# A sandwich layer (attention, then a ternary feed-forward) on one core: the feed-forward's splits turned by VectorE and HBM, two V units and one product moved, identity transposes at the start

## The chip, the cores and the metric

The kernel runs on one core of a Trainium2 chip. The metric is device time in microseconds (us) of one execution. Before the change it is 1528.37 us, the median of 3 runs (1528.33 to 1528.66).

## What is computed

The input x has two batches of 1024 rows of 512. W_Q, W_K and W_V have 16 heads of 128 x 512, W_O 16 of 512 x 128; w1 and w3 are 1365 x 512, w2 is 512 x 1365. All are fp32.

```python
def ternary_quant(w):
    s = mean(abs(w))
    return clip(round(w / s), -1, 1) * s          # as far as the value goes

def attn(x):                                      # causal, 16 heads of 128
    q, k, v = (einsum('bsd,hed->bhse', x, W) for W in (W_Q, W_K, W_V))
    s = einsum('bhse,bhme->bhsm', q, k) / sqrt(128), masked above the diagonal
    return einsum('bhse,hde->bsd', softmax(s) @ v, W_O)

def ffn(x):
    return (silu(x @ w1q.T) * (x @ w3q.T)) @ w2q.T   # w1q = ternary_quant(w1), ...

x = x + layernorm(attn(layernorm(x)))
out = x + layernorm(ffn(layernorm(x)))
```

## The kernel before, in words

**Numbers.** TensorE multiplies in a fast fp32 form of reduced precision, so most operands are split into a leading and a low part (and in attention a third, their difference form), and a product is the sum of two or three matmuls. Such parts are called forms here: `xb` are those of x, `qa`, `ql`, `qd` (also k, v, o) those of the weights, `za`, `zl`, `zd` those of the heads' outputs, `gh`, `gl` those of the hidden values. Scores (L555) and products with V (L649) run in plain fp32, which is two instructions for each.

**Start (L674 to L712).** The loads of x and of the first weights go out. VectorE and ScalarE normalise the rows of batch 0, tile by tile of 128 rows. `block_unit` (L392) turns a tile: four TensorE transposes against the identity (L402) into PSUM, then ScalarE (L406), VectorE (L407) and VectorE or POOL (L408) make its three forms. The first four tiles go through, then the query and key units of head 0 (L461), then V units.

**Attention.** There are N = 32 heads (16 in each batch), two to a pair g, with 8 steps i each, one for each tile of 128 query rows. The order is written out by hand in the loop at L796. Step i issues the scores of three steps ahead (`look`, L771: L555, causal mask L560, row maximum L564, exp L571, scaling L577), fill work for the next head (query and key units L470 and L477, V units L498, output units L518), and a product with V. A V unit (`value_unit`, L487) does two of the eight tiles of a pair in 24 matmuls of 256 columns; there are four for a pair. For a product, P must be transposed: VectorE turns blocks of 32 x 32 (L603), the blocks go to HBM (`hop<-blocks`, L614) and come back at their places in four reads (`pt<-hop`, L630). Two steps are turned together: product (n, m) covers steps 2m and 2m+1 of head n, and `product` (L767) says at which step it is issued: two steps after the second of them, three where that is step 7. In the last head the steps run in the order 4, 5, 6, 7, 0, 1, 2, 3, and the first three hidden units of the feed-forward are put in at steps 2, 4 and 6 (`early_hidden`, L777).

Raw weights come by `load_raw` (L414). The raw tile of V has the buffer of the difference form `vd` (tag "vd"), and those of Q and K the buffers of `qd` and `kd`. All DMAs are issued by SyncE in one queue, in order (SPq in the profile): a DMA that waits holds up those behind it. L835 loads the raw V of the next pair at step 1, L438 and L439 make its forms at steps 3 and 4, L445 at steps 5 and 6.

**Feed-forward.** There are four blocks (b, tb) of 512 rows, each with NF = 11 steps f over the hidden size. In step f the loop at L991 issues the hidden unit of two steps ahead (`hidden`, L309: 16 matmuls L317, Silu L325, VectorE L328, gh by ScalarE L333, gl by VectorE L334), then the down product of step f (L915: 8 matmuls into four PSUM accumulators), and three pieces of `middle`, the closing of batch 1's attention (in block 1 only). The block's input must be split ahead of its first hidden unit, which is issued at step 9 of the block before. `split_unit` does that for one tile of 128 rows at steps 4, 6, 7 and 8: load of the row tile (batch 0, L237), normalisation by VectorE (L123), four TensorE transposes into PSUM (L255), leading part by ScalarE (L257), low part by VectorE (L258). Block 1's splits were done in head N-2 in the same way. PSUM tiles named `mm` (tag "mm", four buffers) are shared by hidden units, splits, products and V units. After step 10, `finish` normalises the four sums, adds the residual (POOL, L939; for batch 0 from `res` loads) and stores out.

`tc.issue_after(i)` and `past(i)` put what follows behind instruction i in the order in which the program issues.

Of the kernel before, what the change touches and what calls it, by code (L numbers as in the profile page):

```python
# [9 lines left out]
FP = mybir.dt.float32  # L10
# [25 lines left out]
def sandwich_kernel(  # L36
# [85 lines left out]
    def normalise(dst, src, mv, r, t):  # L122
        return nc.vector.tensor_scalar(  # L123
            dst, src, mv[:, t, 0:1], r[:, t : t + 1], ALU.subtract, ALU.mult
        )
# [103 lines left out]
    def split_units(b, tb, t, stage):  # L229

        tt = tb * QT + t
        held = {}

        def load():
            held["x"] = xt = stage.tile([P, D], FP, name="xt")
            if b == 0:
                nc.sync.dma_start(xt, mid0[ts(tt, P), :])  # L237

        def normal():
            src = held["x"] if b == 0 else acc[:, tt, :]  # L240
            normalise(held["x"], src, mv_mid[b], r_mid[b], tt)

        return load, normal, lambda: split_turn(b, tb, t, held["x"])

# [92 lines left out]
    with ExitStack() as att:  # L337
# [91 lines left out]
        def lead_and_low(kind, n, part, first=False):  # L429

            if (kind, n) not in weights:
                weights[kind, n] = [form(kind, "a"), form(kind, "l")]
            lead, low = (w[:, part] for w in weights[kind, n][:2])
            raw = wraw[kind, n][:, part]
            if first:
                nc.vector.tensor_scalar(lead, raw, LEAD, None, ALU.mult)
            else:
                nc.scalar.mul(lead, raw, LEAD)  # L438
            nc.gpsimd.tensor_tensor(low, raw, lead, ALU.subtract)  # L439

        def difference_form(kind, n, part):
            if len(weights[kind, n]) == 2:
                weights[kind, n].append(form(kind, "d"))
            lead, low, diff = (w[:, part] for w in weights[kind, n])
            nc.vector.scalar_tensor_tensor(diff, low, -T12, lead, ALU.mult, ALU.add)  # L445
# [235 lines left out]
        @contextmanager  # L681
        def past(*instructions):
            with ExitStack() as order:
                for i in instructions:
                    order.enter_context(tc.issue_after(i.ins))
                yield

        def normal_pair(t):
            for k in (t, t + 1):
                row_stats(mv_in[0][:, k, :], acc[:, k, :])  # L690
            std_unit(0, t, 2)
            return [normal_unit(0, k) for k in (t, t + 1)]

        with past(*normal_pair(0)):
            done = normal_pair(2)
        with past(*done):
            for kind in range(2):
                lead_and_low(kind, 0, EVERY, first=True)
            blocks = [block_unit(0, t) for t in range(QT)]
        lead, low, diff = blocks[-1]  # L700
        with past(diff):
            for kind in range(2):
# [64 lines left out]
        product = {}  # L767
        for at, (n, i) in enumerate(order):
            if i % 2 == 1:
                product[at + (3 if i == NT - 1 else 2)] = n, i // 2  # L770
        def look(idx):  # L771
            if idx < len(order):
                live[order[idx]] = scores(*order[idx])
# [22 lines left out]
        for n in range(N):  # L796
            g, j = divmod(n, 2)
            b, pr = divmod(g, NP)

            fill = [[] for _ in range(NT)]  # L800

            def put(steps, units):
                for i, u in zip(steps, units):
                    fill[i].append(u)

            if n + 1 < N:
                units = [
                    lambda k=k, kind=kind: query_key_unit(n + 1, kind, k)()
                    for k in range(2)
                    for kind in range(2)  # L810
                ]
                late = {2 * NP - 1: (6, 7), N - 2: (5, 5)}.get(n, (5, 6))
                put((3, 4) + late, units)
            if j == 1 and g + 1 < G:
                units = [lambda u=u: value_unit(g + 1, u) for u in range(QT)]
                put((0, 1, 6, 7) if n != 2 * NP - 1 else (0, 1, 5, 6), units)
            if n == 0:
                put((1, 7), [lambda u=u: value_unit(0, u) for u in (2, 3)])
            if j == 0 and g > 0:
                outs = output_units(g - 1)  # L820
                put((0, 0, 0, 1, 4, 5, 6, 7), outs)
            for t in range(NT):
                if divmod(block_at + t, NT)[0] == n:
                    put([(block_at + t) % NT], [lambda t=t: block_unit(1, t)])
            for t in range(QT):
                if divmod(split_at + t, NT)[0] == n:
                    put([(split_at + t) % NT], splits[t][2:])
            if n == N - 1:
                put((2, 4, 6), [lambda f=f: early_hidden(f) for f in range(EARLY)])
            for i in range(NT):  # L830
                idx = n * NT + i
                with behind("turn", of=idx + 1):
                    if n + 2 < N and i > 5:
                        load_raw(i - 6, n + 2)
                    if j == 0 and g + 1 < G and i == 1:  # L835
                        load_raw(2, g + 1)
                    if j == 1 and i == 1:
                        load_raw(3, g)
                    if n == N - 2 and i >= NT - EARLY:
                        f = i - NT + EARLY  # L840
                        load_t13(f, wpool.tile([P, 2, D], FR, name=("va", "vd", "vl")[f]))
                todo = fill[i]
                for u in todo[:2]:
                    with past(newest[0]):
                        u()
                rest = None
                if idx in product:
                    with past(newest[0]):
                        rest = values(*product.pop(idx))
                for u in todo[2:]:  # L850
                    with past(newest[0]):
                        u()

                with behind("max", "half", "exp", of=idx + 1):
                    if n + 1 < N and i in (2, 3):
                        difference_form(i - 2, n + 1, EVERY)
                    if n + 1 < N and i in (1, 2):
                        lead_and_low(i - 1, n + 1, EVERY)
                    at = g + 1 - j
                    if at < G and i in (3, 4):  # L860
                        lead_and_low(2 + j, at, (FRONT, BACK)[i - 3])
                    if at < G and i in (5, 6):
                        difference_form(2 + j, at, (FRONT, BACK)[i - 5])
                with past(newest[0]):
                    look(idx + AHEAD)
                if rest:
                    with behind("max"):
                        rest()
                if idx + 2 < len(order):
                    with behind("max"):  # L870
                        turn(*order[idx + 2])
                        if idx + 3 == len(order):
                            bring(*next(iter(blocks_of)))
                with behind("max", "half", "turn"):
                    for u in side[idx]:
                        u()
# [8 lines left out]
    with ExitStack() as ffn:  # L885
# [56 lines left out]
        def finish_last(b, tb, t):  # L942
# [18 lines left out]
            for u in (t, t - 1) if t == QT - 1 else (t - 1, t):  # L961
# [7 lines left out]
                eng.tensor_tensor(y, y, acc[:, tt, :], ALU.add)  # L969
                nc.sync.dma_start(out[b, ts(tt, P), :], y)  # L970

        last = {}
        square = small.tile([P, 1], FP, name="square", bufs=1)
        nc.vector.tensor_tensor(square, scales[2][:, 2:3], scales[2][:, 2:3], ALU.mult)
# [15 lines left out]
        middle += third[NT - 1 :]  # L990
        for n, (b, tb, f) in enumerate(steps):  # L991
            after = n // NF + 1
            if f in (4, 6, 7, 8) and after < len(steps) // NF:
                nb, ntb, _ = steps[after * NF]
                split_unit(nb, ntb, (4, 6, 7, 8).index(f), xpool)
            end = after == len(steps) // NF
            if end and f == NF - 4:
                ffn_hidden(*steps[n + 2])
                ffn_hidden(*steps[n + 3])
            elif EARLY <= n + 2 < len(steps) and not (end and f == NF - 3):  # L1000
                ffn_hidden(*steps[n + 2])
            if end and f >= NF - 2:
                if f == NF - 1:
                    for t in range(QT):
                        down(b, tb, NF - 2, [t])
                        down(b, tb, NF - 1, [t])
                        finish_last(b, tb, t)
                continue
            down(b, tb, f)
            with tc.issue_after(lows[-2]):  # L1010
                for u in middle[:3]:
                    u()
            middle = middle[3:]
            if f == NF - 1:
                finish(b, tb)
# [43 lines left out]
```

## Time and profile before

| | us |
|---|---|
| median of 3 runs | 1528.37 |
| the profiled execution | 1527.27 |
| its span, first to last instruction | 1525.5 |
| TensorE (PE) busy | 1479.8 (97%) |
| VectorE (DVE) busy | 1071.9 (70%) |
| ScalarE (ACT) busy | 792.7 (52%) |
| GpSimd (POOL) busy | 402.4 (26%) |
| DMA engines, share of the span | 57.5% |

Where TensorE's time lies: 14 us pass before the first product of the projections, attention ends at about 1279 us, the feed-forward's matmuls end at 1515.3 us, and the last normalisation and stores take the rest. In four stretches of 200 us or less:

| stretch, us | TensorE busy | VectorE busy | DMA share |
|---|---|---|---|
| 200 to 400 | 200.0 | 155.8 | 0.67 |
| 600 to 800 | 192.0 | 151.6 | 0.73 |
| 1200 to 1290 | 85.6 | 66.7 | 0.64 |
| 1400 to 1450 | 50.0 | 22.1 | 0.09 |

How to read the lines: a timeline line gives start, duration, engine, line of the kernel, operation, out<-in with shapes, number of instructions, and in brackets the idle time before it with what ended it. A line of waits gives who waited for whom: us in total, times, the longest. The chain is followed back from the last instruction, at each step to what released it. PE is matmul time, PEld weight loads beside it. The granted clock is a share of full speed. Matmul ends are modelled and overlap the next start, so starts are compared here rather than durations.

### The profile page before, as it was taken

The numbers are of one execution on the slowest core, as the hardware profiler recorded it, in microseconds if no ns is written. First come the engines' busy times: TensorE is split into PE (matmuls) and PEld (weight loads), VectorE is DVE, ScalarE is ACT, GpSimd is POOL, SyncE is SP. The second block draws the span as 40 slices with busy tenths as digits, with TensorE's granted clock in tenths as the row PEclk, the third lists the DMA queues.
The fourth block names the chain that finished last, engine by engine and source line by source line (L and its number), as shares of the span: only waits on it lengthen the run. The fifth ranks groups of instructions, "written<-read, shape, count | busy, mean of one in ns | idle before, by whom it ended". The sixth has DMA issues, their size and how long they took to land.

```text
span 1525.5 us, 21249 instructions
## 1 busy us (share of the span) xinstructions
PE 1479.8 (97%) x7078; PEld 1188.0 (78%) x7078; DVE 1071.9 (70%) x2111; ACT 792.7 (52%) x1566; POOL 402.4 (26%) x472
## 2 busy tenths in 40 slices
PE   7899999999999999999999999999999999999997
PEld 5687878787878787777787878787777868788885
DVE  7667686868786878687777777777777776555344
ACT  4556555555555555666664545454545465344232
POOL 3122222222222233434433333333222110210010
PEclk9999999999999999999999999999999999999999
DMA  3566767676766675768766666666665677210000
GB/s 122 180 177 179 205 177 206 181 206 182 203 190 171 182 208 181 205 165 249 236 201 190 196 190 195 191 193 193 184 180 167 191 202 239 75 56 15 28 28 28
DMA packets 171252, 257.26 MB, mean 169 GB/s; under 512 B 18228, under 2 KB 113460, under 8 KB 167048
## 3 DMA queue, kind: packets, MB, share of 16 engines
q1 hardware_dynamic: 171144, 255.90, 57.5%
q8 instruction: 57, 0.93, 0.2%
q14 instruction: 51, 0.42, 0.1%
HBM read 157.28 MB, written 98.56 MB: 168 GB/s over the span
## 4 chain that ended last, share of the span: by engine, by line
PE 69%; issue 9%; DVE 8%; DMA 5%; ACT 5%; POOL 2%; SPq 0%; DVEq 0%; POOLq 0%; ACTq 0%
PE mm L649 12%; PE mm L470 11%; PE s_ps L555 11%; PE mm L317 10%; PE mm L498 9%; PE mm L518 6%; PE mm L477 5%; PE yp L915 4%; DVE nm L564 2%; ACT p_sb L571 2%; DMA hop<-blocks 2%; DMA wqk<-wk 1%; POOL kl L439 1%; DVE blocks L603 1%; DMA xt<-x 1%
## 5 line engine op out<-in xcount | busy, mean ns | idle before, releaser
L571 ACT ACTIVATE p_sb<-s_ps,nm 128x128 f32<-128x128 f32 (+7 forms) x256 | 189.9, 742 | 367.3 <-DVE nm L564 363.7
L555 PE MATMUL s_ps<-k,q 128*128 128x512 f32 (+3 forms) x768 | 289.7, 486 | 0.7 <-ACT p_sb L571 0.7
L649 PE MATMUL mm<-pt,v_sb 128*128 128x256 f32 (+1 forms) x1280 | 273.2, 361 | 16.6 <-ACT va L438 5.7
L649 PEld LDWEIGHTS mm<-pt,v_sb 128*128 128x128 f32 x1280 | 239.4, 191 | 53.7 <-ACT q L453 6.4
L577 ACT ACTIVATE p_sb<-p_sb,ri 128x128 f32<-128x128 f32 (+7 forms) x256 | 197.8, 773 | 31.8 <-DVE ri L576 29.2
L564 DVE TENSOR_REDUCE nm<-s_ps 128x1 f32<-128x128 f32 (+7 forms) x256 | 193.7, 757 | 7.1
L603 DVE STREAM_TRANSPOSE blocks<-p_sb 128x128 f32<-128x128 f32 (+7 forms) x256 | 197.1, 770 | 1.1 <-ACT p_sb L577 0.9
L555 PEld LDWEIGHTS s_ps<-k,q 128*128 128x128 f32 x768 | 132.2, 190 | 69.3 <-issue 61.4
L669 POOL TENSOR_TENSOR zd<-za,zl 128x256 fp32r<-128x256 f32 x128 | 94.5, 738 | 325.9 <-DVE zl L666 317.0
L560 DVE TENSOR_TENSOR s_ps<-s_ps,causal 128x128 f32<-128x128 f32 x256 | 75.4, 295 | 137.2 <-PE s_ps L555 136.5
L498 PE MATMUL mm<-va,xb 128*128 128x256 f32 x512 | 158.6, 310 | 0.0
L498 PE MATMUL mm<-vd,xb 128*128 128x256 f32 x512 | 144.9, 283 | 1.2 <-POOL xb L408 0.9
L498 PE MATMUL mm<-vl,xb 128*128 128x256 f32 x512 | 144.6, 282 | 0.0
L470 PE MATMUL mm<-xb,qa 128*128 128x512 f32 x256 | 119.7, 467 | 1.4 <-ACT xb L406 1.4
L470 PE MATMUL mm<-xb,ka 128*128 128x512 f32 x256 | 112.6, 440 | 0.4 <-ACT zf L661 0.4
L498 PEld LDWEIGHTS mm<-vl,xb 128*128 128x128 f32 x512 | 97.7, 191 | 7.1 <-issue 4.1
L498 PEld LDWEIGHTS mm<-va,xb 128*128 128x128 f32 x512 | 97.7, 191 | 7.1 <-issue 3.4
L470 PE MATMUL mm<-xb,ql 128*128 128x512 f32 x256 | 101.8, 398 | 0.0
L470 PE MATMUL mm<-xb,kl 128*128 128x512 f32 x256 | 101.3, 396 | 0.3 <-POOL kl L439 0.3
L498 PEld LDWEIGHTS mm<-vd,xb 128*128 128x128 f32 x512 | 97.7, 191 | 1.6 <-POOL xb L408 1.1
L600 POOL MEMSET blocks<- 128x128 f32 x128 | 26.0, 204 | 265.6 <-DMA hop<-blocks 194.7
L532 DVE TENSOR_TENSOR acc<-acc,mm 128x512 f32<-128x512 f32 x128 | 86.1, 683 | 12.4 <-ACT acc L527 5.2
(157 smaller groups left out, 2771.1 us busy)
## 6 DMA issues: line engine op xcount, KB each, us to landing
hop<-blocks SPq DMA_DIRECT2D x32, 1024.0 KB, 4.5
pt<-hop SPq DMA_DIRECT2D x128, 256.0 KB, 5.9
hop<-blocks SPq DMA_DIRECT2D x32, 768.0 KB, 3.4
pt<-hop SPq DMA_DIRECT2D x128, 192.0 KB, 3.8
hop<-blocks SPq DMA_DIRECT2D x32, 512.0 KB, 3.2
pt<-hop SPq DMA_DIRECT2D x128, 128.0 KB, 3.1
wqk<-wq SPq DMA_DIRECT2D x32, 256.0 KB, 5.1
wqk<-wk SPq DMA_DIRECT2D x32, 256.0 KB, 6.5
```

Of the source, the lines that this page charges most:

```text
L317: newest[0] = nc.tensor.matmul(ps[:fl, :], lhsT=t[:, c, :], rhs=bl[k][:, c, :], start=(c == 0 and k == 0), stop=(c == NC - 1 and k == 1),)
L470: newest[0] = nc.tensor.matmul(main, lhsT=forms[f][0][:, c, :], rhs=forms[f][1][:, c, :], start=(c == 0 and f == 0), stop=(c == NC - 1 and ...
L498: newest[0] = nc.tensor.matmul((main, main, diff)[f][:, ts(t, 2 * P)], lhsT=forms[f][0][:, c, token], rhs=forms[f][1][:, c, :], start=(t = ...
L518: newest[0] = nc.tensor.matmul((main, main, diff)[f], lhsT=zs[g, t // QT, j][f][:, ts(t % QT, P)], rhs=weights[3, g][f][:, 2 * j : 2 * j + ...
L532: nc.vector.tensor_tensor(dst, dst, diff, ALU.subtract)
L555: newest[0] = nc.tensor.matmul(s_ps[:, ds(k0, kl)], lhsT=proj[n, 0, i // QT][:, ts(i % QT, P)], rhs=proj[n, 1, k0 // TB][:, :kl], start=Tr ...
L564: top = nc.vector.tensor_reduce(nm, s_ps[:, :L], axis=AX.X, op=ALU.max, negate=True)
L571: e = nc.scalar.activation(p_sb[:, :L], s_ps[:, :L], AF.Exp, bias=nm, accum_out=rs)
L577: nc.scalar.mul(p_sb[:, :L], p_sb[:, :L], ri)
L603: turned = nc.vector.transpose(b[:, :, 0 : i + 1, il, :].rearrange("p to t r -> p t to r"), p_sb[:, :L].rearrange("p (b r) -> p b r", r=32),)
L649: newest[0] = nc.tensor.matmul(dst, lhsT=proj[g, 2][:, kt, ts(j, P)], rhs=rhs, start=(kt == 0), stop=(kt == 2 * m + 1),)
L669: nc.gpsimd.tensor_tensor(diff, lead, low, ALU.subtract)
```

## The change

Four parts; line numbers of the changed kernel are 1 higher from L243 on, 17 or 18 higher in the attention loop and 53 higher in the last loop's body.

Part A: a PSUM tile `idle` is taken, and TensorE transposes the identity into it 20 times before the first tile of x, 8 times after the second tile and 3 times after the fourth.

Part B: V units 2 and 3 of head 0 stand at steps 1 and 2 in place of 1 and 7. In head 0 the load of the next raw V stands at step 2 in place of 1, and its forms one step later.

Part C: in the last head the product of steps 4 and 5 (i = NT - 3 = 5) is issued three steps after, in place of two. At its new step the second early hidden unit stands ahead of it.

Part D: the splits of blocks 2 to 4 go through VectorE and HBM, in four stages at different steps: load at steps 1 to 4, normalisation, 32 x 32 transposes and store at steps 2 to 5, four reads back at steps 3 to 6, leading and low part at steps 5 to 8 (tile 0 first). The transposes of TensorE and their PSUM tiles are gone there.

```diff
@@ split_units
         def normal():
             src = held["x"] if b == 0 else acc[:, tt, :]
             normalise(held["x"], src, mv_mid[b], r_mid[b], tt)
+            return held["x"]
@@ the start
+        idle = ps_m.tile([P, P], FP, name="idle", tag="mm")
+
+        def busy(times):
+            with ExitStack() as order:
+                if newest[0] is not None:
+                    order.enter_context(past(newest[0]))
+                for _ in range(times):
+                    newest[0] = nc.tensor.transpose(idle, ident, ident)
+
+        busy(20)
         with past(*normal_pair(0)):
             done = normal_pair(2)
         with past(*done):
             for kind in range(2):
                 lead_and_low(kind, 0, EVERY, first=True)
-            blocks = [block_unit(0, t) for t in range(QT)]
+            blocks = []
+            for t in range(QT):
+                blocks.append(block_unit(0, t))
+                if t % 2 == 1:
+                    busy((8, 3)[t // 2])
@@ attention
             if i % 2 == 1:
-                product[at + (3 if i == NT - 1 else 2)] = n, i // 2
+                late = i == NT - 1 or (n == N - 1 and i == NT - 3)
+                product[at + 2 + late] = n, i // 2
...
             if n == 0:
-                put((1, 7), [lambda u=u: value_unit(0, u) for u in (2, 3)])
+                put((1, 2), [lambda u=u: value_unit(0, u) for u in (2, 3)])
...
-                    if j == 0 and g + 1 < G and i == 1:
+                    if j == 0 and g + 1 < G and i == 1 + (n == 0):
                         load_raw(2, g + 1)
...
-                    if at < G and i in (3, 4):
-                        lead_and_low(2 + j, at, (FRONT, BACK)[i - 3])
-                    if at < G and i in (5, 6):
-                        difference_form(2 + j, at, (FRONT, BACK)[i - 5])
+                    form_step = i - 3 - (n == 0)
+                    if at < G and form_step in (0, 1):
+                        lead_and_low(2 + j, at, (FRONT, BACK)[form_step])
+                    if at < G and form_step in (2, 3):
+                        difference_form(2 + j, at, (FRONT, BACK)[form_step - 2])
@@ feed-forward
+        def split_stages(b, tb, t):
+            load, normal, _ = split_units(b, tb, t, xpool)
+            if t == 0:
+                split[b, tb] = [xblocks.tile([P, NC, TB], FR, name="xb") for _ in range(2)]
+            held = {}
+
+            def turn():
+                xs = xpool.tile([P, 4, NC, 32], FP, name="xs", bufs=2)
+                nc.vector.transpose(
+                    xs.rearrange("p to c r -> p c to r"),
+                    normal().rearrange("p (b r) -> p b r", r=32),
+                )
+                held["d"] = d = dram.tile([P, 4, NC, 32], FP, name="hopx", bufs=2)
+                nc.sync.dma_start(d, xs)
+
+            def read():
+                held["u"] = u = xpool.tile([P, 4, NC, 32], FP, name="xu", bufs=2)
+                for to in range(4):
+                    nc.sync.dma_start(
+                        u[ts(to, 32)].rearrange("x a c r -> x a (c r)"),
+                        held["d"][:, to].rearrange("(a x) c r -> x a (c r)", a=4),
+                    )
+
+            def forms():
+                u = held["u"]
+                hi, lo = (
+                    part[:, :, ts(t, P)].rearrange("p c (a r) -> p a c r", a=4)
+                    for part in split[b, tb]
+                )
+                nc.scalar.copy(hi, u)
+                nc.vector.tensor_tensor(lo, u, hi, ALU.subtract)
+
+            return load, turn, read, forms
...
-            if f in (4, 6, 7, 8) and after < len(steps) // NF:
+            if f == 0 and after < len(steps) // NF:
                 nb, ntb, _ = steps[after * NF]
-                split_unit(nb, ntb, (4, 6, 7, 8).index(f), xpool)
+                stages = [split_stages(nb, ntb, t) for t in range(QT)]
...
             down(b, tb, f)
+            if after < len(steps) // NF:
+                for at, stage in zip((1, 2, 3, 5), range(4)):
+                    if 0 <= f - at < QT:
+                        with tc.issue_after(lows[-2]):
+                            stages[f - at][stage]()
```

In the changed kernel the store of a split is L1004, its reads L1009, the leading part L1020, the low part L1021, the transposes by VectorE L999, the identity transposes L703; L317 becomes L318, L649 L650, L915 L933.

## Prediction, on record before the changed kernel was run

> **What bounds the kernel now.** I read the busy times first, then TensorE's waits, then the chain in the stretches where it waited longest, then the timeline around the lines that the change touches. The busy line says that TensorE is the bound nearly everywhere (1525.5 - 1479.8 = 45.7 us without a matmul, some 10 of them behind the last matmul at 1515.3):
>
> ```profile
> PE 1479.8 (97%) x7078; PEld 1188.0 (78%) x7078; DVE 1071.9 (70%) x2111; ACT 792.7 (52%) x1566; POOL 402.4 (26%) x472
> ```
>
> So a gain is either a wait of TensorE that goes, or matmul time that goes. Its waits, longest in total first (engine, line, releaser: us, times, longest):
>
> ```profile
> PE tr L402 <- ACT acc L387: 7.7, 2, 7.3
> PE mm L649 <- ACT va L438: 5.7, 1, 5.7
> ...
> PE mm L649 <- DMA pt<-hop: 2.9, 1, 2.9
> ...
> PE trx L255 <- DVE xt L123: 1.0, 1, 1.0
> ...
> PE yp L915 <- DVE gl L334: 0.6, 1, 0.6
> ```
>
> The first is the start, which no part of the change shortens before 7.27. The other four lie where the change works. The chain between 61 and 75 us shows the 5.7:
>
> ```profile
> 61.81 2.88 PE mm L498 x24
> 64.69 0.02 SPq L422
> 64.72 0.03 issue
> 64.75 4.52 DMA wvo<-wv
> ...
> 69.35 0.64 ACT va L438
> 69.98 0.40 issue
> 70.39 4.53 PE mm L649 x12
> ```
>
> SyncE's own waits in that stretch name the same place: L422 waited 5.7 us for L498. The raw V weights of pair 1 go into the buffer of the difference form of pair 0, which the last V unit of head 0 (step 7) still reads; the load stands in the SP queue from 59.04 to 64.75, and the fourth read of the block (0,2) behind it. The product (0,2) at 70.39 needs that read. After the gap the clock is halved: the granted clock is 0.50 from about 67.5 to 74.25, and the 12 matmuls take 4.52 us, against 1.52 us for 8 at 56.9, so 2.3 for 12.
>
> **Part B, V units of head 0 at steps 1 and 2.** The 24 matmuls (2.88 us) move from step 7 to step 2. They need x blocks and V forms that are there by 31 us. The load of the next raw V moves to step 2, right behind them, and its forms (ACT L438, POOL L439, DVE L445) one step on, to steps 4 to 7. Gone are 70.39 - 64.69 = 5.70 of wait and 4.52 - 2.4 = 2.1 of half clock: 7.8.
> What is late next: the products themselves, for TensorE now comes to (0,2) at 64.7. Its transposes follow the score of step 6, which ends 2.9 later than before, so the store leaves at 52.6 + 2.9 = 55.5. Store to first read 3.3 (171.10 to 174.41), to the fourth read 1.36, its landing 4.26 (1245.40 to 1249.66): 64.4. The product (0,3) is due at 83.24 - 7.8 = 75.4; its store waits for VectorE at 63.65, then 4.9 to 5.0 to the reads (179.79 to 184.71), 1.36, and 4.3 to 5.9 to land: 74.2 to 75.9. At worst, with the 6.67 that this store took at 65.67 to 72.34, 77.6. I take 0.2 of new wait: **-7.6**, between -4.6 (a wait of 1 and one of 2.2) and -7.8. Also moved: the SP queue gets the 512 KB load ahead of the reads of (0,1), which are due at 59.7 and issue at 51 at the latest.
>
> **Part C, product (31,2) behind the second early hidden unit.** TensorE stands 2.86 us before 1249.79, for reads issued at 1244.04 to 1245.8. In the new order score, 16 matmuls of L317 (3.63) and then the product follow 1246.9, so the reads are in time. The work up to the product of the next block (1249.79 to 1261.11, 11.3 us) then ends at 1258.25. But that block's reads issue at 1252.07 to 1253.8 whatever TensorE does, and DMA traffic stops at 1259.0: a wait of 0.8 takes the place of the 2.86. ScalarE's next Silu, which frees the PSUM of the third hidden unit, needs exp, a table load of 1.28 and then 0.69, and is done near 1253.1, 3 us ahead of its reader. **-2.0**, between -1.0 (a landing 1 us later) and -2.86.
>
> **Part D, splits of blocks 2 to 4.** One step of the feed-forward is 24 matmuls, and a split makes it longer:
>
> ```profile
> 1355.22 3.79 PE L317 MATMUL mm<-xb,oa 128*128 128x512 f32 x16
> 1360.67 0.60 PE L255 MATMUL trx<-ident,xt 128*128 128x128 f32 x4
> 1361.02 3.90 PE L317 MATMUL mm<-xb,ol 128*128 128x512 f32 x16
> 1366.58 3.79 PE L317 MATMUL mm<-xb,od 128*128 128x512 f32 x16
> 1372.03 0.60 PE L255 MATMUL trx<-ident,xt 128*128 128x128 f32 x4
> ```
>
> Steps without a split are 5.44 apart (1327.97 to 1333.41). Here the six steps from 1355.22 to 1389.76 hold four splits and take 34.54 in place of 32.65: 0.47 each, 0.36 of it ahead of the next hidden unit and the rest in its first matmuls. 12 splits give 5.7. In block 1 the 1.01 before L255 (1302.45) goes with it: it hung on ACT, POOL L285 and a load issued only at 1298.97. So does the 0.58 before L915 (1299.55): there three down products stood in a row ahead of the transposes, and in the new order each follows two hidden units behind its own. Sum 7.2.
> Added are 12 DVE transposes of 128x512 (L603 takes 0.57 to 0.70 for that size), 12 stores of 256 KB and 48 reads of 64 KB (pt<-hop of 64 KB lands in 2.0), and the subtraction now reads SBUF (as L334, 0.69). VectorE is busy 19 to 22 of 50 us there, the DMA engines under 0.11: all of it lies beside matmuls. New waits: the store behind the transpose and the reads behind the store hold the SP queue, behind which stand out<-y, res and xt loads; ScalarE's copy and VectorE's subtraction wait in line for the reads, with Silu, gh and gl behind them. A down product needs gl two steps on, so these may stand some 5 us unseen. The deadline is the next block's first hidden unit at step 9. By rows, for block 1 (times of before): transposes at 1299, 1301, 1304.5 and 1310; the last reads wait for the second xu buffer (subtraction at 1314), issue to 1316, land by 1318; ScalarE copies them at 1321, VectorE subtracts at 1322.9 to 1323.6, behind sg of step 10; TensorE comes at 1324. That is 0.4 to spare, and a subtraction beside POOL can take double (1.37 for two at 1298.12, 1.29 each on POOL): a wait of up to 1. In blocks 2 and 3 the last subtraction stands ahead of that sg, with steps to spare. I take 0.3: **-6.9**, between -5.0 (0.55 a block and the 0.58 staying) and -7.3.
>
> **Part A, identity transposes.** 31 transposes from about 1.5 us, when the identity is there. The rows that decide:
>
> ```profile
> 10.97 1.97 PE L402 MATMUL tr<-ident,acc 128*128 128x128 f32 x8 [1.76 <-DVE xb L407]
> ...
> 18.91 0.63 PE L470 MATMUL mm<-xb,ka 128*128 128x512 f32 x1
> 19.34 0.54 PE L470 MATMUL mm<-xb,kl 128*128 128x512 f32 x1
> 19.71 0.40 PE L470 MATMUL mm<-xb,ka 128*128 128x512 f32 x1
> 19.95 0.39 PE L470 MATMUL mm<-xb,kl 128*128 128x512 f32 x1
> ```
>
> Matmuls start 0.427 apart up to 19.34 and 0.23 apart from 19.71: half clock until about 19.6, although the granted clock prints 1.00 there. If TensorE is at full clock by 10.97, the 8 transposes take 1.03 (as at 24.88) and the chain behind them (ACT L406 at 12.98, then VectorE to 29) starts 0.7 earlier. The 14 slow matmuls could give 14 x 0.195 = 2.7, but from 13.6 to 28.4 the chain is VectorE's, and they lie beside it. If the clock stays low, 8 x 0.246 = 1.97 behind 9.21 ends at 11.18: 0.2 lost, and 3 more cost TensorE 0.3 at 13.6. The nearest row for packed work is the restart at 70.39, where the clock rose after 3.9 us. New transposes fill 1.5 to 13.6 with no gap above 1 us, so I take **-0.7**, between -2.7 and +0.3.
> The Trainium skill, TensorE: Matmul & The Clock Gate, Part 4: PE-mode transpose, speaks against this: transposes do not count as busy for the clock gate, and full rate does not engage for them. No run here shows transposes alone; that 10.97 to 13.6 had little effect agrees with it. By that rule the part is +0.2.
>
> **Sum.** -0.7 - 7.6 - 2.0 - 6.9 = -17.2. The profiled execution took 1527.27 (span 1525.5 and 1.77 around it), so 1510.1. The median of the runs, 1528.37, is 1.1 above the profiled one; on that level 1528.37 - 17.2 = **1511.2**.
>
> **Rivals.**
> 1. The transposes do not raise the clock. For: 2 x 8 of them before 13 did not, and matmuls needed to 19.6. Against: those had gaps of 1.76 and 0.69. Part A is +0.2: 1512.1. Chance 0.35.
> 2. Attention's waits only change their name: products (0,2) and (0,3) wait for their reads, and block 3 of the last head lands a microsecond later. For: I find margins of 0.3 and -0.5 us. Against: no product after 72 us waits for a read but one. B -4.6, C -1.0: 1528.37 - 0.7 - 4.6 - 1.0 - 6.9 = 1515.2. Chance 0.12.
> 3. Slower: the splits come too late. Store, reads, out and res share one queue in order; if reads stand there behind out<-y, which waits for POOL, the first hidden unit of each block waits for its last form. It decides from the point where the last reads land after step 9 begins; the change is lost when that wait passes 17.2 / 3 = 5.7 a block, one whole step. With 8 a block, 1528.37 - 17.2 + 24 = 1535.2. For: 60 more DMAs on a queue that blocked 5.7 us at 59. Against: two to three steps of slack by the rows above. Chance 0.04.
>
> **Chances.** Forecast 0.47, rival 1 0.35, rival 2 0.12, rival 3 0.04, the remaining 0.02 a partial rival 3 near no change. Range: all gains at their best give 1528.37 - 20.8 = 1507.6; the upper bounds (+0.3 - 4.6 - 1.0 - 5.0 = -10.3) give 1518.1. I take 1507.5 to 1518.0. 0.2% is 3 us, about what a measurement of this kernel can tell from no change. Faster by more: forecast, rivals 1 and 2, 0.94; within: 0.02; slower: rival 3, 0.04.
>
> **What would show it.** B: no wait of L650 above 1 us before 80, granted clock 1.00 there. C: L318 twice ahead of the product, a wait near 0.8 before the next. D: no L256 in the feed-forward, steps of 5.44 throughout, no wait of L318 at the start of a block. A: matmuls 0.23 apart from the first one at about 13. Wrong would be a wait of L318 on the subtraction L1021, or one of L650 on pt<-hop longer than 2.

## The result, and the profile after

The changed kernel takes 1513.14 us (median of 5 runs, 1511.27 to 1516.63) against 1528.66 beside it; the ratio is 0.9896, 95% interval 0.9881 to 0.9911. A second set gave 1511.93 (4 runs) and 0.989 (0.9875 to 0.9905). The forecast was 1511.2, between 1507.5 and 1518.0. The total was right; most of its terms were not, and their errors cancelled, so that it came out this near is in part luck.

The profiled execution took 1511.27, with a span of 1509.5, which is 16.0 shorter than that of before. From its page, the busy times:

```profile
PE 1475.6 (98%) x7061; PEld 1184.9 (78%) x7061; DVE 1080.6 (72%) x2123; ACT 792.7 (53%) x1566; POOL 404.3 (27%) x472
```

TensorE now stands without a matmul for 33.9 us (1509.5 - 1475.6) in place of 45.7; some 6 of these 11.8 are the identity transposes (4.53, 1.04 and 0.49 at the start), which count as busy. Its waits (engine, line, releaser: us, times, longest):

```profile
PE tr L403 <- ACT acc L388: 2.8, 3, 1.2
PE mm L650 <- DMA pt<-hop: 2.7, 3, 1.9
...
PE mm L650 <- issue: 1.3, 2, 1.0
```

The 5.7 behind L438 is gone, and so are L255 and the wait of the down product on `gl`. But L650 waits for its reads three times in place of once, and "issue", twice, is a new name: the timeline has products (0,2) and (0,3) there, which come right behind the landing of their reads.

To see where each part paid, I cut both traces at five instructions: VectorE's first L407 (L408 in the changed kernel), the last transposes of batch 0's second four tiles, the product (1,0), the score of query tile 0 of the last head, and the first and the last down product.

| stretch | part | before | after | moved | forecast |
|---|---|---|---|---|---|
| first L407 (10.23 in both) to the last start transposes | A | 18.99 | 18.77 | -0.22 | -0.7 |
| to product (1,0) | B | 61.15 | 55.06 | -6.09 | -7.6 |
| to the score at 1238.99 (1232.04) | none | 1148.62 | 1147.98 | -0.64 | 0 |
| to the first down product | C | 39.64 | 38.78 | -0.86 | -2.0 |
| to the last down product | D | 236.30 | 228.51 | -7.79 | -6.9 |
| to the end | none | 10.57 | 10.17 | -0.40 | 0 |

**B.** The chain between 64 and 77 us of the changed kernel:

```profile
64.47 0.24 issue
64.70 2.62 PE mm L650 x12
...
71.69 2.87 PE mm L499 x24
74.56 1.08 PE s_ps L556 x4
75.64 1.04 issue
76.68 3.37 PE mm L650 x15
```

The gap of 5.7 and the half clock are gone (2.62 for 12 matmuls, 4.53 before), and the product (0,3) now waits 1.04.

**C.** The chain that leads to the end of attention, in the changed kernel:

```profile
1239.38 1.26 DVE blocks L604
...
1240.69 4.99 DMA hop<-blocks
...
1247.58 5.88 DMA hop<-blocks
...
1254.83 1.98 DMA pt<-hop
1256.80 0.35 issue
1257.15 0.89 PE mm L650 x4
...
1260.75 2.85 DMA pt<-hop
1263.61 0.14 issue
1263.74 1.75 PE mm L650 x8
```

It holds no product before 1257: from VectorE's turn at 1239.38 on it is stores and reads, each behind the other on SyncE's queue. TensorE's side of it, with 1.88, 0.63 and 0.21 of waiting:

```profile
1246.96 4.20 PE L318 MATMUL mm<-xb,vl 128*128 128x512 f32 x16
1253.04 3.48 PE L650 MATMUL mm<-pt,v_sb 128*128 128x256 f32 x16 [1.88 <-DMA pt<-hop]
1257.15 0.89 PE L650 MATMUL mm<-pt,v_sb 128*128 128x256 f32 x4 [0.63 <-DMA pt<-hop]
...
1263.74 1.75 PE L650 MATMUL mm<-pt,v_sb 128*128 128x256 f32 x8 [0.21 <-DMA pt<-hop]
```

Before, two products of the last head stood: (31,2) for 2.86 and the last one, (31,1), for 0.91:

```profile
1271.57 1.75 PE L649 MATMUL mm<-pt,v_sb 128*128 128x256 f32 x8 [0.91 <-DVE acc L529]
```

So the printed waits of this stretch fell from 3.77 to 2.72.

**D.** TensorE's timeline in block 1, where it stood for 0.58 and 1.01 before:

```profile
1288.96 3.79 PE L318 MATMUL mm<-xb,ol 128*128 128x512 f32 x16
...
1294.40 3.79 PE L318 MATMUL mm<-xb,od 128*128 128x512 f32 x16
...
1299.84 3.79 PE L318 MATMUL mm<-xb,t 128*128 128x512 f32 x16
```

Steps of 5.44 (a few of 5.47) with no wait, from the first step to the last.

### The profile page after: what moved, and what is told of

Read it like the earlier page. It is cut to its first block, busy times and chain, and to the rows that moved or that the text cites. A ratio compares the mean times of both kernels' runs of the same rounds, so it can differ in the third digit from the quotient of the medians.

```text
span 1509.5 us, 21335 instructions
## 1 busy us (share of the span) xinstructions
PE 1475.6 (98%) x7061; PEld 1184.9 (78%) x7061; DVE 1080.6 (72%) x2123; ACT 792.7 (53%) x1566; POOL 404.3 (27%) x472
## 4 chain that ended last, share of the span: by engine, by line
PE 66%; issue 10%; DVE 9%; DMA 7%; ACT 5%; POOL 2%; SPq 1%; DVEq 0%; POOLq 0%; ACTq 0%
PE mm L650 11%; PE mm L471 10%; PE mm L318 10%; PE s_ps L556 10%; PE mm L499 8%; PE mm L519 6%; PE yp L933 5%; PE mm L478 5%; DVE nm L565 3%; DMA hop<-blocks 2%; ACT p_sb L572 2%; DMA wqk<-wk 2%; ACT p_sb L578 1%; POOL kl L440 1%; DVE blocks L604 1%
## 5 line engine op out<-in xcount | busy, mean ns | idle before, releaser
L650 PE MATMUL mm<-pt,v_sb 128*128 128x256 f32 (+1 forms) x1280 | 271.7, 359 | 11.3 <-ACT q L454 3.7
L650 PEld LDWEIGHTS mm<-pt,v_sb 128*128 128x128 f32 x1280 | 238.1, 190 | 48.8 <-ACT q L454 6.2
```

The lines of the kernel that those rows point to most:

```text
L650: newest[0] = nc.tensor.matmul(dst, lhsT=proj[g, 2][:, kt, ts(j, P)], rhs=rhs, start=(kt == 0), stop=(kt == 2 * m + 1),)
```

## The experiments

**Each part alone on the kernel before**, one set on one chip (before there: 1528.92, median of 23 runs, 1526.28 to 1530.99). The edits are the pieces of the change's diff.

Part A alone:

```diff
+        busy(20)
...
+                if t % 2 == 1:
+                    busy((8, 3)[t // 2])
```

> The kernel before with part A alone (20, 8 and 3 identity transposes at the start). Theory: the identity transposes do raise TensorE's clock, so the two sets of eight real transposes take 1.1 to 1.25 each instead of 1.94 and 1.97, but from 13.5 us on the chain is VectorE's and the later transposes (29.22 before) move by 0.2 to 0.3 only; whole time -0.2, not to be told from no change. Rival, the forecast's term: the 0.7 won at 12.98 stays to the end, so 28.5 for those transposes and -0.7 on the time.

Measured: 1529.06, ratio 0.9998 (0.999 to 1.0007). TensorE's timeline of this run:

```profile
6.84 1.97 PE L402 MATMUL tr<-ident,acc 128*128 128x128 f32 x8 [0.86 <-ACT acc L387]
8.61 1.84 PE L701 MATMUL idle<-ident 128*128 128x128 f32 x8
10.64 1.25 PE L402 MATMUL tr<-ident,acc 128*128 128x128 f32 x8 [0.20 <-DVE xb L407]
...
16.45 0.39 PE L470 MATMUL mm<-xb,kl 128*128 128x512 f32 x1
17.41 1.17 PE L477 MATMUL mm<-xb,qd 128*128 128x512 f32 x4 [0.57 <-DVE qd L445]
19.10 1.17 PE L477 MATMUL mm<-xb,kd 128*128 128x512 f32 x4 [0.52 <-DVE kd L445]
```

Full clock came at about 10.6, after 36 transposes (28 of the identity) and no other matmul, and from 13.7 on the matmuls of L470 were 0.23 apart: the last stands at 16.45, against 19.95 before. Then TensorE stood before L477 for VectorE's `qd` and `kd`, and the stretch of part A took 18.78 in place of 18.99. The time alone can't tell -0.2 from -0.7 (the interval is -1.5 to +1.1); the trace can, and the theory holds: VectorE sets the end of the stage. VectorE's timelines show where its own lead went, first before, then with part A alone:

```profile
14.21 2.84 DVE L408 TENSOR_TENSOR xb<-xb 128x512 fp32r<-128x512 f32 x2
16.98 1.76 DVE L445 SCALAR_TENSOR_TENSOR qd<-ql,qa 128x512 fp32r<-128x512 f32 x1
18.66 0.68 DVE L445 SCALAR_TENSOR_TENSOR kd<-kl,ka 128x512 fp32r<-128x512 f32 x1
```

```profile
13.17 2.39 DVE L408 TENSOR_TENSOR xb<-xb 128x512 fp32r<-128x512 f32 x2
15.49 1.78 DVE L445 SCALAR_TENSOR_TENSOR qd<-ql,qa 128x512 fp32r<-128x512 f32 x1
17.18 1.77 DVE L445 SCALAR_TENSOR_TENSOR kd<-kl,ka 128x512 fp32r<-128x512 f32 x1
```

VectorE reached `qd` 1.49 earlier (0.33 of it because this execution started earlier), but `kd` now lay beside POOL's L439, which ran from 14.97 to 18.40, and took 1.77 in place of 0.68. The next form, `vd`, began at 18.88 in place of 19.26, which leaves 0.05: what was won was given back within one instruction.

Part B alone:

```diff
-                put((1, 7), [lambda u=u: value_unit(0, u) for u in (2, 3)])
+                put((1, 2), [lambda u=u: value_unit(0, u) for u in (2, 3)])
...
-                    if j == 0 and g + 1 < G and i == 1:
+                    if j == 0 and g + 1 < G and i == 1 + (n == 0):
                         load_raw(2, g + 1)
...
+                    form_step = i - 3 - (n == 0)
```

> The kernel before with part B alone (V units 2 and 3 of head 0 at steps 1 and 2, raw V load and forms one step later). Theory: the 5.70 wait and the 2.1 of halved clock go, but the products (0,2) and (0,3) then wait about 0.2 and 1.0 for their own reads, so -6.0 to -6.3 at product (0,3) and in the time. Rival, the forecast's term: waits of 0.2 in all, -7.6; it would mean that the waits seen in the changed kernel come from the other parts.

Measured: 1520.07, ratio 0.9951 (0.9935 to 0.9967), so -7.5 with 2.5 either way. In the trace, waits of 0.20 and 1.11 ahead of (0,2) and (0,3), and 55.09 in the stretch of part B, -6.06: the waits are B's own, and the theory's number holds.

Part C alone:

```diff
-                product[at + (3 if i == NT - 1 else 2)] = n, i // 2
+                late = i == NT - 1 or (n == N - 1 and i == NT - 3)
+                product[at + 2 + late] = n, i // 2
```

> The kernel before with part C alone (product of steps 4 and 5 of the last head one step later). Theory: the 2.86 wait goes, and the next product waits 1.9 and the one after it 0.6 for their reads; the first down product of the feed-forward comes 0.9 earlier, time -0.9. Rival, the forecast's term: a wait of 0.8 in the next product and none after it, time -2.0.

Measured: 1525.71, ratio 0.998 (0.9971 to 0.9989): -3.1, between -1.7 and -4.4. That is more than the theory's -0.9. The rival's -2.0 lies within the interval, but its single wait of 0.8 is not in the trace, which has 1.59 and 0.37, and 37.76 in the stretch of part C. A reason that fits came out of the sister runs, whose last head is that of before: their stretch took 43.94 (A alone) and 41.45 (B alone) against 39.64 and 39.60 (before, D alone). The two long ones have the clock halved behind the wait ahead of (31,2), which was 3.71 in A alone and 2.86 in B alone. The granted clock of B alone, in slices of 2 us (the figure third from the end), and of before, for the same work:

```profile
1240.00:1242.00 2.00, 0.40 (x2) 0.00 (x0) 1.97 (x4) 1.62 (x5) 0.84 (x1) 1.00 1.06 278
1242.00:1244.00 2.00, 0.74 (x4) 0.69 (x5) 1.27 (x4) 1.48 (x4) 1.64 (x3) 1.00 1.04 396
1244.00:1246.00 2.00, 2.00 (x7) 1.63 (x6) 0.00 (x0) 0.00 (x0) 1.25 (x2) 0.62 0.29 123
1246.00:1248.00 2.00, 2.00 (x7) 1.44 (x5) 0.00 (x0) 0.66 (x2) 0.00 (x0) 0.52 0.65 188
```

```profile
1246.00:1248.00 2.00, 0.93 (x6) 0.50 (x4) 1.67 (x2) 2.00 (x6) 0.30 (x1) 1.00 1.08 232
1248.00:1250.00 2.00, 0.21 (x1) 0.24 (x2) 1.79 (x6) 1.25 (x5) 1.64 (x2) 1.00 1.05 345
1250.00:1252.00 2.00, 2.00 (x10) 1.77 (x10) 0.00 (x0) 0.40 (x1) 1.59 (x2) 1.00 0.58 238
```

B alone and before both waited 2.86. One ran at half clock for 3.41 us behind it, the other not at all. So the profile of before from which I forecast shows the cheap form of this wait.

Part D alone (`split_stages` and the loop that calls its four stages):

```diff
-            if f in (4, 6, 7, 8) and after < len(steps) // NF:
...
+                for at, stage in zip((1, 2, 3, 5), range(4)):
```

> The kernel before with part D alone (splits of blocks 2 to 4 by VectorE and HBM). Theory: 12 splits at 0.48 each (5.76) and the two waits of block 1, start to start 2.03, go with no new wait: -7.8 between the first and the last down product, and in the time. Rival, the forecast's term: -6.9, with the rest of what the changed kernel won lying elsewhere (a last transfer that landed 0.4 sooner).

Measured: 1521.14, ratio 0.9947 (0.9935 to 0.9959), -8.1 with 1.8 either way; first to last down product 228.61, -7.69. The theory holds.

The four ratios together make -19.0, with 3.6 either way if their errors are independent. That is more than the -15.9 of the whole change, but not outside the errors.

**Is it the clock?** Two waits of the kernel before are filled with work that produces nothing.

```diff
+        def busy(times):
+            idle = ps_m.tile([P, P], FP, name="idle", tag="mm")
+            for _ in range(times):
+                newest[0] = nc.tensor.transpose(idle, ident, ident)
+        gaps = {(0, 2): 40, (N - 1, 2): 18}
...
+                    if product[idx] in gaps:
+                        with past(newest[0]):
+                            busy(gaps[product[idx]])
```

> The kernel before, with identity transposes put into two of its waits and nothing else: 40 (5.2 us at 0.13) ahead of the product (0,2), 18 (2.3) ahead of the product (31,2) of the last head. They take no wait away. Theory: a gap of TensorE of some 3 us or more halves the granted clock for one or more stretches of 3.4 us behind it, in every execution behind the 5.7 and in some behind the 2.9, and transposes count as work for it. Then product (0,2) runs its 12 matmuls in 2.4 to 2.6 in place of 4.5 to 5.0, product (0,3) comes 2.1 earlier, the mean clock is 0.996 to 0.997 in most executions, and the median is 2.5 to 4 lower. Rival: transposes do not count; the clock is 0.50 behind 68 us as before, and the time is the same. Second rival: the clock is not the cause of the spread, so -2.1 and the same spread.

Measured: 1526.88 against 1528.68, ratio 0.9987 (0.9976 to 0.9998), so -2.0, between -0.3 and -3.7. TensorE's timeline:

```profile
64.31 4.53 PE L787 MATMUL idle<-ident 128*128 128x128 f32 x40
70.11 2.62 PE L649 MATMUL mm<-pt,v_sb 128*128 128x256 f32 x12 [1.28 <-issue]
```

The product (0,2) starts where it started before, at 70, but its 12 matmuls take 2.62 in place of 4.53, the granted clock is 1.00 there, and the stretch of part B takes 59.17 in place of 61.15: 1.98 of the 2.1 of half clock, apart from the wait. Transposes alone held the clock, and the rival that they do not is out. The mean clock of the runs rose from between 0.992 and 0.996 to between 0.996 and 0.998. The spread did not shrink: 1524.97 to 1531.1, and the two slowest had a mean clock of 0.997. These are the numbers of the second rival, -2.1 and the same spread: the halved clock behind (0,2) costs time in every profile that keeps the wait, but that it makes the spread is not shown. In the last head the clock held too, but the product (31,2) began 1.1 later after the start of its stretch than before, still behind its reads, and that stretch took 40.84; this may be why the total is less than expected.

**What makes (0,3) wait?** Two looks at the changed kernel with less traffic between its store and its reads.

```diff
-                    if n + 2 < N and i > 5:
+                    if n + 2 < N and i > 5 and n > 0:
                         load_raw(i - 6, n + 2)
+                    if n == 1 and i == 0:
+                        load_raw(0, 2)
+                        load_raw(1, 2)
```

> The changed kernel with the two loads of raw Q and K for head 2 (256 KB each, issued at 63.95 and 64.41 between the store and the reads of product (0,3)) put off to head 1, behind those reads. Theory: they share the DMA engines (0.99 busy from 65 to 70) with the reads, whose last one takes 6.5 to land; without them the store takes 4 in place of 4.9 and the wait of 1.04 ahead of product (0,3) is gone: -1.0 to -1.3 there. Rival: the wait hangs on VectorE's late turn at 63.5 and on the reads' own 1 MB, and stays within 0.4.

Measured: 1512.3, ratio 0.9888 (0.9872 to 0.9905). The wait at (0,3) is gone; store to first read is 4.46 (63.09 to 67.55) in place of 4.91. Two loads of L148 moved up into the place of the two that left, so the traffic there fell from some 740 to 455 KB. But at 80.97 TensorE waits 0.44 for POOL's `ql`, made of the raw Q that now comes late, the wait ahead of (0,2) is 0.37, and the stretch of part B takes 55.26 in place of 55.06. In this one profile the wait went with the two loads, and nothing is won: it changed its name.

```diff
         side = [[] for _ in range(N * NT)]
-        at = 0
+        at = 8
```

> The changed kernel with all side work of the weight scan (loads L148 of 227 KB and what follows) started one head later, so that head 0 has none of these loads: one of them is issued at 65.32 between the store and the reads of product (0,3), two at 70.83. Theory, as for the raw Q and K loads: less traffic beside the reads, the 1.04 wait goes to 0.3 or less. Rival: the traffic that counts is raw Q and K, or none, and the wait stays at 0.7 to 1.1. The rest of attention carries the same work at other steps, so its time may move by some tenths either way.

Measured: 1514.15, ratio 0.9903 (0.9884 to 0.9921). The wait did not go: (0,3) starts at 76.83, behind 2.03. TensorE came to it 0.84 sooner, and it began 7.0 after the issue of its four reads of 256 KB had ended (69.78), no less than the 6.5 of the changed kernel. Behind the wait the clock was halved: 16 matmuls took 5.17 in place of 3.48, and the stretch of part B took 57.25. The rival holds: these loads were not what held it up.

**What held part C?** Output units are put into the waits of the last head. The last difference form of W_O is made whole at step 5, so that it is there for them.

```diff
+                outs = output_units(G - 1)
+                put((6,), [lambda: (outs[4](), outs[5]())])
...
+                    if n == N - 1 and form_step == 2:
+                        difference_form(3, at, EVERY)
...
-        for u in outs[QT:]:
-            u()
+        for t in (6, 7, 0, 1):
+            outs[t]()
         (last,) = product.values()
         values(*last)()
-        for u in outs[:QT]:
-            u()
+        for t in (2, 3):
+            outs[t]()
```

> The changed kernel, with the output units of two row tiles put ahead of the product (31,3), two more ahead of (31,1), and the difference form of the last W_O made in one piece a step earlier. Theory: what part C did not win is a chain of DMAs (store 4.99, reads, store 5.88, reads) that begins with VectorE's turn at 1239.38 and doesn't follow TensorE; only work put into its waits (1.88, 0.63 and 0.21 printed, 2.9 start to start) wins them. First down product 1.5 to 2.7 earlier than 1270.8, time -1.5 to -2.7. Rival: the output units wait for PSUM (four tiles, the third hidden unit's are read by VectorE until 1253.2), so the wait changes its name and the gain is under 0.5.

Measured: 1510.65 (1510.27 to 1512.29), ratio 0.9882 (0.9865 to 0.9899). TensorE's timeline around the products that had waited:

```profile
1247.76 4.20 PE L318 MATMUL mm<-xb,vl 128*128 128x512 f32 x16
1251.80 0.61 PE L519 MATMUL mm<-oa,za 128*128 128x512 f32 x2
...
1254.36 0.62 PE L519 MATMUL mm<-od,zd 128*128 128x512 f32 x2
1254.82 4.06 PE L650 MATMUL mm<-pt,v_sb 128*128 128x256 f32 x20
...
1264.68 1.74 PE L650 MATMUL mm<-pt,v_sb 128*128 128x256 f32 x8
```

No product of the last head waits (one output unit does, 0.31 for POOL's `zd`); the stretch takes 36.99 in place of 38.78. The theory holds at the lower part of its range, and the rival of full PSUM is out.

**A last set on one chip** (before: 1528.79): the changed kernel again, the one with the moved output units again, the same without part A, and one on part D.

> The changed kernel once more, beside the variants of this set. Theory: 1511 to 1514, mean clock 0.996 to 0.998. Nothing else is expected of it.

Measured: 1511.93 (1511.28 to 1512.68), ratio 0.989 (0.9875 to 0.9905).

> The changed kernel with four output units moved into the waits of the last head, once more, now beside the changed kernel itself. Theory: the waits of 1.88, 0.63 and 0.21 are filled, so 1.8 to 2.7 faster than the changed kernel. Rival: the two differ by less than 0.5, and what was seen before was the spread.

Measured: 1510.35 (1509.11 to 1511.08), ratio 0.9879 (0.9864 to 0.9893). Against the changed kernel beside it -1.6, a little under what was expected, and the ranges of the two do not touch, though the intervals of their ratios do. No product of the last head waits here either, but at 1273.70 TensorE stands 0.41 for a load (`t<-tern`), which no profile of the changed kernel shows; the next kernel has 0.54 of it. So a part of the gain was lost again behind the stretch.

> The kernel with the moved output units, without any identity transpose at the start. Theory: part A moves the stage's end by 0.1 to 0.25 only, because VectorE sets it, so the time is that of the kernel with them, within 0.5. Rival: 0.7 or more slower, the forecast's term for part A.

```diff
-        busy(20)
...
-                if t % 2 == 1:
-                    busy((8, 3)[t // 2])
```

Measured: 1509.94 (1509.58 to 1510.69), ratio 0.9878 (0.9863 to 0.9892). The theory holds: without part A nothing is lost. The stretch of part A is 18.89 here. Over all profiles it is 18.83 to 18.99 without the part and 18.77 to 18.87 with it. This kernel has the lowest median of the study, though its range overlaps that of the one with part A.

```diff
-                for at, stage in zip((1, 2, 3, 5), range(4)):
+                for at, stage in zip((1, 2, 4, 5), range(4)):
```

> The changed kernel with the reads of the splits (third stage) one step of the feed-forward later, the forms where they were: the condition of the rival that forecast a slower kernel. In the changed kernel the last subtraction of block 1 ends 0.2 before the matmul that reads it, those of blocks 2 and 3 4.3 before. Theory: block 1's last reads land some 3 later, and the first hidden unit of the next block waits 0.5 to 2 once; blocks 2 and 3 wait for nothing; time +0.5 to +2. Rival: the reads are not what comes last (ScalarE copied at 1313.4, the subtraction stood behind VectorE's own gate product until 1315.3), so no wait and no change.

Measured: 1511.43, ratio 0.9887 (0.987 to 0.9903). One wait appears, at the place that was expected, 0.19 as printed:

```profile
1316.10 0.39 PE L318 MATMUL mm<-xb,va 128*128 128x512 f32 x1
1316.67 3.71 PE L318 MATMUL mm<-xb,va 128*128 128x512 f32 x15 [0.19 <-DVE xb L1021]
```

From start to start that step took 5.94 in place of 5.44, so the wait costs 0.50; first to last down product is 229.01 in place of 228.51, and the time can't be told from that of the changed kernel. That is the lower edge of the theory's size, but not its cause. ScalarE copied the last tile at 1313.31, as in the changed kernel (1313.38): the last read landed 2.4 later (1312.19 against 1309.84) and still 1.1 before the copy. What moved is the subtraction, which took 1.40 in place of 0.69. It lay beside POOL's L286 (1313.53 to 1316.07), which in the changed kernel had ended at 1315.42, just behind the start of the subtraction. On the cause the rival is nearer: the reads had time to spare, VectorE only 0.2.

## Why the prediction was right, point by point

- **Bound and sum.** That a gain is a wait of TensorE that goes, or matmul time that goes, held in every run. The sum of -17.2 came out as -16.0 between the profiles and -15.5 between the medians. Two slips move nothing: the best case adds up to 20.7, not 20.8, and 0.57 is what L603 takes for 128x384 (0.70 for 128x512).
- **A, -0.7: the size failed, 0.1 to 0.2 measured.** The clock did rise, and rival 1 is out as a mechanism, though its 1512.1 is nearer to the first median than the forecast. The step that failed is "the chain behind them starts 0.7 earlier": it did, and VectorE's next form gave it back beside POOL. The mark I set (matmuls 0.23 apart from the first) held from the fourth matmul on in five of the eight profiles with part A. In the other three, that of the changed kernel among them, the clock fell again, at 11.2 to 13.1, and some of the matmuls were 0.43 apart. The stage took 18.77 to 18.87 in all eight.
- **B, -7.6: -6.1 measured.** The 5.70 went, and 1.9 of the 2.1 (2.62 for 12 matmuls in place of 4.53). The failed term is "0.2 of new wait": it was 0.24 and 1.04, so the mark "no wait above 1 us" failed too (1.14 in the second profile). The store of (0,3) and the issue of its reads came as worked out (63.50, 4.91, 1.32). The landing, which I took to be 4.3 to 5.9, was 6.7, from 69.73 on. The 5.9 was no upper end: it is the median of these reads on the page of before, and its trace has one of 7.3 at 226.7.

```profile
pt<-hop SPq DMA_DIRECT2D x128, 256.0 KB, 5.9
```

- **C, -2.0: -0.86 in the profile, about -2.4 over several.** The wait of 0.8 in place of 2.86 was 1.88 and 0.63, for the store took 4.99 and the one behind it 5.88, against the 4.9 and 4.4 of before from which I had read the landing. The sign I had set for being wrong, a wait of L650 on `pt<-hop` longer than 2, came in the second profile of the changed kernel (2.09 at 1253.88). Two terms that I left out work the other way. The 0.91 ahead of (31,1) shrank to 0.21. And the 2.86 costs a halved clock in some executions: without the part the stretch is 39.60 to 43.94 (four profiles, mean 41.16), with it 37.76 to 39.59 (six, mean 38.75; in two of these the new wait, there 2.1, halved the clock).
- **D, -6.9: -7.79 measured.** The splits cost some 5.7 as worked out. That leaves 2.1 for the two waits of block 1, which were entered at their printed 1.6. From start to start they are longer (0.97 from 1298.58 and 1.40 from 1301.05, where neighbours are 0.23 apart), since matmul ends are modelled past the next start. And the 0.3 of new wait did not come: the subtraction of double length that I had allowed for (the row at 1298.12 is one instruction of 1.37) is seen at a block's end only in the run with the later reads. Rival 3 did not come either: no block start waited in any run but that one, and there 0.5.
- **Rival 2** was right in its two conditions: both products of head 0 wait for their reads, and the last head's product lands a microsecond late. Its price for B (-4.6) was too small, and D made up for the rest. The first median, 1513.14, lies about as near to its 1515.2 as to my 1511.2; the second, 1511.93, is nearer to mine.
- **The 0.64 between** the parts is scatter: that stretch took 1147.6 to 1150.9 in five profiles with the work of before. **The 0.40 at the end**, behind the last store's issue, is seen in all profiles with part D (10.1 to 10.2) and in none without (10.3 to 10.6). Why stays open; no run was made for it.

## What to carry to other kernels

Price a wait by what follows it as well: a gap that is long enough to halve the clock costs up to 1.7 us more for each stretch of 3.41 (half of it), and whether it does so changes from execution to execution, so that one profile may show the cheap form. Take the upper end of a landing from the longest rows of its size, not from their median. Before counting a gain at the start of a chain, follow it through the next engine that is never idle, and ask what runs beside each of its instructions at the new time. And where stores and reads follow each other on one queue, moving the consumer moves the wait; only work put into the wait wins it.

## What the runs showed of the hardware

- **The clock is halved for stretches of 3.41 us, at a phase that differs from run to run.** Between the first and the last matmul, low stretches measured 3.41 (B alone behind 1244.5; the filled waits behind 616.8; C alone behind 618.6) or 6.83 (A alone behind 1249.3; before behind 67.4). In the four kernels that keep the wait of 5.3 to 5.7 ahead of (0,2), the clock fell 2.4, 2.7, 4.1 and 5.0 after its beginning. A gap of 2.86 was followed by a low stretch in one execution and by none in another. The stretch behind 616.8 followed no long gap, but one of 0.90 and one of 1.27 within a few us. What decides between the two outcomes was not tried; that a gap costs nothing when it lies across the end of a stretch is a guess that no run tests. The Trainium skill, TensorE: Matmul & The Clock Gate, Part 1, "What's actually happening", gives a free-running window of 3413 ns; the traces agree with its length. The Trainium skill, the same page, "HAM oscillation", warns of gaps above some 3.4 us; here 2.0 to 2.9 were enough.
- **Transposes count for the clock.** 40 identity transposes held it through a wait of 5.8 us. With part A, where TensorE does nothing but transposes until 12.4, eight of them that began at 10.6 or before took 1.25 or less in all eight profiles, against 1.94 and 1.97 before; without it the matmuls were 0.43 apart until 17.7 or later, in six. The Trainium skill, the same page, Part 4: PE-mode transpose, says that full rate does not engage for them; these runs differ from it, and the measurement decides.
- **VectorE beside POOL.** The same 128x512 form (L445) took 0.68 after POOL had ended and 1.77 beside POOL's L439. The subtraction L1021 took 0.69 and, beside L286, 1.40.
